# Deformable convolution: a third tap sampled by hat matrices, and ScalarE weighting one of four neighbours

## The chip, the cores and the metric

The kernel runs on one core of a Trainium2 chip. Its engines are TensorE (PE in the profile; its weight loads are shown as PEld), VectorE (DVE), ScalarE (ACT), GpSimd (POOL) and SyncE (SP). Each engine works through its own queue of instructions in order; they meet through semaphores. The metric is the device time of one execution in microseconds (us), lower is better.

## The reference

The whole program is a network of four layers on an image batch `x` of 4 x 128 channels x 64 x 64 positions. The change touches one of its operations only, the deformable convolution of layer 1, which is added to its input after a layer norm over the channels. For each of nine taps k of a 3x3 window, each position has an offset (dy, dx) and a mask, both made by ordinary convolutions; the input is sampled at the shifted position by bilinear interpolation, and the samples are convolved:

```python
off = conv2d(x, w_off, b_off)                       # dy, dx for each of 9 taps
mask = sigmoid(conv2d(x, w_mod, b_mod))
py = oh + ky + dy ;  px = ow + kx + dx
y0 = floor(py) ; x0 = floor(px) ; wy = py - y0 ; wx = px - x0
sampled = v00*(1-wy)*(1-wx) + v01*(1-wy)*wx + v10*wy*(1-wx) + v11*wy*wx
sampled = sampled * mask
out = einsum('bckhw,ock->bohw', sampled, weight) + bias
```

`v00` to `v11` are the four neighbours of the shifted position, zero outside the image. All data are float32.

## The kernel before, in words

**Order of the program.** Phases run one after another: an involution, a recurrence, the deformable convolution, an expert layer, a convolution, a second expert layer, an attention and a last expert layer. The deformable convolution runs from about 1237 to 2453 us of the profiled span. Its work is written between `with tc.manual_schedule(engines=ORDERED)` and the end of the function `deformable`: there each engine's queue has the instructions in the order in which the Python code issues them, so generators that are advanced by `next` set what stands beside what.

**Tiling.** 128 channels lie on the partitions when whole images are held (`xs`, 4 x 4096 positions). An image is cut into 8 chunks of 512 positions, a chunk into 4 tiles of 128. Loops: batch b (4), chunk c (8), gathered tap k (the list `BY_ASK`), pair of tiles i (2). The body of the innermost loop is one step: `taken`, then `step()`.

**Gathered taps.** Seven of nine taps (all but 3 and 4) are gathered. For a pair of tiles `taken` (L993) issues two indirect DMAs from GpSimd (L998); each brings, for 128 positions, the four neighbours' 128 channels from a table in DRAM into a tile `dcn_g` (eight buffers, `GATHERED`). VectorE then multiplies all four neighbours of both tiles by their weights (L1006); the weights of two chunks stand in PSUM (`near_w`, copied at L1160). Two steps' counts later `joined` (L1009) transposes each neighbour on TensorE into one PSUM bank, adding up the four (L1015, 8 joins a pair), so that channels lie on the partitions. When a tap's four tiles are done, `turn_back` (L1118) lets ScalarE copy the bank to `dcn_st` (L1120), and `convolve` (L1123) multiplies by the tap's 128x128 weights into the chunk's output bank (L1127). After the last tap `finish` (L1133) adds it to `xs` on VectorE (L1135). The lags are written in `at(lag, ...)`: join in the step after the gather's, copy three steps after the second pair's, convolution two steps later, finish one more.

**Hat taps.** Taps 3 and 4 (`HATS`) are sampled without a gather by the generator `hats` (L1036), one for each chunk. A tap's sample is written as products with hat functions max(0, 1-|distance|) between a position and the rows and columns near it. `pieces` holds, for each position, a tap's column position and six row weights, each split in three bf16 parts; TensorE transposes them (L1071) and ScalarE copies them to `rowt` (L1075). A small bf16 matmul (`picked`, L1040) spreads one of these rows over 128 partitions in a bank tagged "by"; `across` and `bent` make the column's hat on ScalarE (L1046, L1049, 512 elements each), `weighted` multiplies it on VectorE by the row hat of one of three neighbouring tiles (L1054), which gives a 128x512 square, and `sampled` multiplies four tiles of it on TensorE by `folded` (L1062), which is the image already multiplied by that tap's weights. `fold` (L1027) makes `folded` for one tile: a matmul of the image's tile with the weights of all hat taps side by side (L1030, also in a bank "by") and a scaled copy on ScalarE (L1034). Five tiles are folded ahead of a batch's first chunk, the others at the end of each chunk's generator.

**The plan of the next batch.** A generator `plan(b + 1)` runs beside batch b: layer norm, the offset convolutions (L840), the table of neighbours in DRAM (L818, L820 and DMAs from SyncE), and `places` (L905), which makes indices, weights and `pieces`. It has 123 turns. `step()` (L1137) counts n up, runs what is due in `later`, advances the plan once, and once more where n is a multiple of five, and then advances the first of the generators of hats in `busy` once.

**PSUM.** All eight banks are held: two for joins ("pt"), one output, "pd" and "pv" for the plan, two "by", one for `near_w`.

## Time and profile before

| quantity | value |
|---|---|
| runs of the kernel (three) | 6048.29 median, 6040.84 to 6049.94 us |
| the profiled execution | 6046.03 us, span 6044.2 us |
| busy share of the span | PE 94%, DVE 72%, ACT 56%, POOL 34% |
| first gather issued, last gather issued | 1308.5 and 2444.1 us |
| in the stage 1308 to 2453 us, busy | PE 1057.6, PEld 783.5, DVE 778.4, ACT 341.3, POOL 852.2 us |
| gathers in it (L998) | 896, mean 0.950 us |
| weighting of four neighbours (L1006) | 448, mean 1.214 us |
| joins (L1015) | 3584 |
| gather, from issue to landing | 3.3 / 3.7 / 7.0 us (least, median, most) |

The profile shows one execution. A row of the time line gives start, duration, engine, line, operation, output and inputs, how many like it were put together, and in brackets how long the engine stood idle before it and what ended that. The end of a matmul is modelled and holds its way through the array, so neighbouring rows of PE overlap; the distance from start to start is what a matmul takes from the next. A table of stretches gives for each stretch its length, the busy time of each engine, the TensorE clock that was granted (1.00 is full), the share of the DMA engines and the rate. A line of the table of waits names who waited, for whom, the sum in us, how often, and the longest.

### The profile page before, as it was taken

How to read it: one execution, taken by the hardware profiler on the slowest of the kernel's cores; microseconds unless marked ns; L12 is line 12 of the kernel's file. 1: busy time of each engine (PE TensorE's matmuls, PEld its weight loads, DVE VectorE, ACT ScalarE, POOL GpSimd, SP SyncE). 2: the span in 40 equal slices, each digit the busy share in tenths (PEclk: the TensorE clock that was granted, in tenths of full speed). 3: DMA queues.
4: the chain of work that ended last, by engine and by line, in shares of the span. 5: the costliest groups of instructions: out<-in, count | busy, mean ns of one | idle time of the engine just before them, and what ended most of it. 6: DMA issues, size and time to landing. Idle time of an engine off the chain costs nothing. (4 is left out here: it accounts for less than half of the span.)

```text
span 6044.2 us, 97814 instructions
## 1 busy us (share of the span) xinstructions
PE 5694.5 (94%) x39923; PEld 2247.6 (37%) x39923; DVE 4381.6 (72%) x4739; ACT 3377.4 (56%) x4224; POOL 2057.5 (34%) x2015
## 2 busy tenths in 40 slices
PE   8999999889999988879969999999999999999799
PEld 2222222446667666343333222322232223222233
DVE  6888887456767676356447788878888888888666
ACT  4444444332323322521427888888888888899421
POOL 3889897027777777200000011111111111111000
PEclk9999999989999999989989999999999999999899
DMA  6434432057777777550365566666666666666200
GB/s 215 98 79 85 94 70 47 1 156 230 215 228 220 230 218 211 166 175 0 104 249 121 130 153 147 136 130 150 149 138 130 149 145 142 130 132 132 60 25 27
DMA packets 273147, 818.40 MB, mean 135 GB/s; under 512 B 42612, under 2 KB 100232, under 8 KB 226600
## 3 DMA queue, kind: packets, MB, share of 16 engines
q0 software_dynamic: 109568, 505.75, 35.2%
q1 hardware_dynamic: 163112, 306.20, 17.6%
q8 instruction: 320, 5.24, 0.4%
q14 instruction: 147, 1.20, 0.1%
HBM read 416.71 MB, written 93.13 MB: 84 GB/s over the span
## 5 line engine op out<-in xcount | busy, mean ns | idle before, releaser
L2020 ACT ACTIVATE att_ex<-att_sc,att_shift 128x1024 f32<-128x1024 f32 x2048 | 2141.5, 1111 | 289.7 <-PE att_sc L2016 172.4
L2051 DVE TENSOR_TENSOR att_dve<-att_dve,att_ex 128x2048 f32<-128x2048 f32 x704 | 1631.5, 2317 | 160.9 <-ACT att_ex L2020 135.3
L2016 PE MATMUL att_sc<-att_q,att_k 32*128 32x512 f32 x8192 | 1290.9, 643 | 8.3 <-ACT att_ex L2020 8.3
L2032 PE MATMUL att_pv<-att_ex,att_vals 128*32 128x512 f32 x8192 | 1095.6, 606 | 0.0
L998 POOL DMA_INDIRECT dcn_g<-dcn_table,dcn_idx x896 | 851.3, 950 | 355.4 <-issue 152.9
L412 DVE SCALAR_TENSOR_TENSOR inv_prod<-inv_pk,bspan,inv_seen 128x512 f32<-128x512 f32 (+1 forms) x1120 | 774.6, 743 | 141.6 <-PE inv_pk L399 141.3
L410 POOL TENSOR_TENSOR inv_prod<-inv_seen,inv_prod 128x512 f32<-128x512 f32 (+1 forms) x672 | 837.5, 1274 | 95.5 <-ACT inv_prod L409 95.5
L2049 POOL DMA_DIRECT2D att_dma<-att_ex x224 | 192.5, 859 | 1980.1 <-ACT att_ex L2020 1707.7
L409 ACT ACTIVATE inv_prod<-inv_pk,bspan 128x512 f32<-128x512 f32 (+1 forms) x672 | 436.1, 682 | 505.2 <-PE inv_pk L399 503.8
L2016 PEld LDWEIGHTS att_sc<-att_q,att_k 32*128 32x128 f32 x8192 | 424.9, 183 | 674.8 <-issue 420.0
L1006 DVE TENSOR_TENSOR dcn_g<-dcn_g,dcn_near_w 128x1024 f32<-128x1024 f32 x448 | 538.8, 1214 | 169.8 <-DMA dcn_g<-dcn_table,dcn_idx 153.9
L399 PE MATMUL inv_pk<-inv_red,wtap 32*96 32x512 f32 (+1 forms) x3584 | 512.2, 637 | 7.4 <-DVE wtap L377 7.4
L1015 PE MATMUL dcn_pt<-ident,dcn_g 128*128 128x128 f32 x3584 | 473.6, 276 | 37.2 <-issue 16.4
L1015 PEld LDWEIGHTS dcn_pt<-ident,dcn_g 128*128 128x128 f32 x3584 | 419.3, 142 | 210.6 <-issue 125.1
L421 PE MATMUL inv_out<-inv_prod,inv_fold 96*32 96x512 f32 (+1 forms) x3584 | 478.5, 606 | 8.5 <-DVE xs L429 8.5
L2032 PEld LDWEIGHTS att_pv<-att_ex,att_vals 128*32 128x32 f32 x8192 | 161.5, 108 | 757.4 <-issue 732.2
L399 PEld LDWEIGHTS inv_pk<-inv_red,wtap 32*96 32x96 f32 (+1 forms) x3584 | 131.8, 170 | 386.7 <-DVE inv_prod L412 362.6
L1034 ACT ACTIVATE dcn_fold<-dcn_pf,dcn_turn 128x256 f32<-128x256 f32 x128 | 60.2, 473 | 365.4 <-PE dcn_pf L1030 365.4
L1120 ACT COPY dcn_st<-dcn_pt 128x512 f32<-128x512 f32 x224 | 129.9, 580 | 239.1 <-PE dcn_pt L1015 239.0
L1127 PE MATMUL dcn_out<-dcn_st,dcn_wk 128*128 128x512 f32 x448 | 236.7, 611 | 21.3 <-DVE xs L1135 21.3
L2521 PE MATMUL top_po<-top_xg,top_we 128*128 128x512 f32 x512 | 233.2, 598 | 0.0
L1054 DVE TENSOR_TENSOR dcn_square<-dcn_hx,dcn_by 128x512 f32<-128x512 f32 x192 | 130.1, 678 | 113.5 <-PE dcn_by L1040 86.2
(433 smaller groups left out, 5371.0 us busy)
## 6 DMA issues: line engine op xcount, KB each, us to landing
att_dma<-att_ex POOLq DMA_DIRECT2D x224, 1024.0 KB, 7.4
inv_seen<-inv_image SPq DMA_DIRECT2D x256, 266.0 KB, 9.1
moe_w<-in_L_ffn_weight SPq DMA_DIRECT2D x64, 1024.0 KB, 14.2
att_dma<-att_ex SPq DMA_DIRECT2D x32, 1024.0 KB, 8.6
att_dve<-att_dma POOLq DMA_DIRECT2D x32, 1024.0 KB
moe_table<-moe_xt SPq DMA_DIRECT2D x64, 288.0 KB, 2.8
dcn_table<-dcn_xt SPq DMA_DIRECT2D x32, 512.0 KB, 4.9
dcn_g<-dcn_table,dcn_idx POOLq DMA_INDIRECT x896, 3.7
```

Source lines behind the costliest of these rows:

```text
L399: nc.tensor.matmul(pk[0:m], wtap[half][rg, i, blk], red[rg, h * CH : (h + 1) * CH], start=True, stop=True)
L409: nc.scalar.activation(prod[0:m, h], pk[0:m], AF.Identity, bias=by)
L410: nc.gpsimd.tensor_mul(of, view, of)
L412: nc.vector.scalar_tensor_tensor(out=of, in0=as_shape(pk[0:m], of), scalar=by, in1=view, op0=ALU.add, op1=ALU.mult)
L421: nc.tensor.matmul(po[CR * blk : CR * (blk + 1), h, :], fold[0:m], prod[0:m, h, :], start=unit == 0, stop=unit == UNITS - 1,)
L998: nc.gpsimd.indirect_dma_start(out=g[:, t, :], out_offset=None, in_=rows, in_offset=bass.IndirectOffsetOnAxis(ap=idx[:, Q4 * c + i + t, k ...
L1006: nc.vector.tensor_mul(near, near, by)
L1015: nc.tensor.matmul(pt[0][:, (i + t) * P : (i + t + 1) * P], near[:, t, q, :], net.ident, is_transpose=True, start=i + t + q == 0, stop=i + ...
L2016: nc.tensor.matmul(pes[h // 2][:, h % 2, :], ks[r, t * P : (t + 1) * P], q[r], start=True, stop=True)
L2020: nc.scalar.activation(ex[:, 2 * two : 2 * two + 2, :], pes[two], AF.Exp, bias=shifts[g][:, two : two + 1],)
L2032: nc.tensor.matmul(block["pv"][r], vals[:, t, r], ex[:, h, :], start=t == 0, stop=t == NT - 1)
L2051: nc.vector.tensor_add(block[who], block[who], ex)
```

## The change

A third tap, 5, is moved from the gathered to the hat taps, so that six are gathered: a chunk has 12 steps and not 14. For the gathered ones ScalarE scales the first of the four neighbours of each tile into a new PSUM bank `first` (one buffer, two tiles of 128); VectorE multiplies the other three by their weights (768 elements and not 1024) and adds `first` to the second neighbour (256 elements), so that a tile has three joins and not four. The new bank is taken from "by", which has one. Gather buffers go from eight to seven, buffers of folds from nine to seven, of squares from four to three. A fold is 384 columns wide and not 256, the pieces have 63 rows and not 42.

The generator of hats is written anew: 9 products and not 6, a row is asked for (`picked`) right before its product and no more one ahead, `sampled` follows two products later and not three, turns with nothing in them stand between, and from the third product on it waits until the output bank of the chunk is there. `step()` advances it twice, before and after the rest, and advances the plan a second time where n is a multiple of five or of two. The last convolution of a chunk first runs what is left of the chunk's generator. In `places` the integer copy of the positions shares the buffer of `over`.

```diff
--- before.py
+++ after.py
@@ -597,7 +597,7 @@

-    HATS, PICKED = (3, 4), 7
+    HATS, PICKED = (3, 4, 5), 7

     def __init__(self, net, one, dram):
         tc, nc, ins = net.tc, net.nc, net.ins
@@ -708,8 +708,8 @@
     HATS, PICKED = sampling.HATS, sampling.PICKED
     NH, H0 = len(HATS), HATS[0]
     BY_ASK = [k for k in range(KK) if k not in HATS]
-    BANKS = {"pt": 2, "out": 1, "pd": 1, "pv": 1, "by": 2}
-    GATHERED = 8
+    BANKS = {"pt": 2, "out": 1, "pd": 1, "pv": 1, "by": 1}
+    GATHERED = 7
     tables, woff, boff = sampling.tables, sampling.woff, sampling.boff
     wk, bias, grids = sampling.wk, sampling.bias, sampling.grids
     with ExitStack() as ctx:
@@ -910,7 +910,7 @@
             pieces = sb.tile([P, NT, NH * PICKED, 3], BF16, name="dcn_pieces", tag="dcn_pieces")
             at = slice(H0, H0 + NH)
             for axis in range(2):
-                pos, low, lowi, over = new("pos"), new("low"), new("lowi", I32), new("over")
+                pos, low, lowi, over = new("pos"), new("low"), new("over", I32), None
                 frac.append(new(f"frac{axis}"))
                 nc.vector.tensor_add(pos, grids[axis], off[:, :, axis : 18 : 2])
                 if axis == 0:
@@ -931,6 +931,7 @@
                 nc.vector.tensor_copy(lowi, pos)
                 nc.vector.tensor_copy(low, lowi)
                 yield
+                over = new("over")
                 nc.vector.tensor_tensor(over, low, pos, ALU.is_gt)
                 nc.vector.tensor_sub(low, low, over)
                 yield
@@ -989,8 +990,9 @@
             )

         near_w = ps.tile([P, 2, Q4, KK, 4], F32, name="dcn_near_w", bufs=1)
-
-        def taken(rows, idx, c, k, i):
+        first = ps.tile([P, 2, P], F32, name="dcn_first", bufs=1)
+
+        def taken(rows, idx, w, c, k, i):


             g = sb.tile([P, 2, 4 * P], F32, name="dcn_g", tag="g", bufs=GATHERED)
@@ -1002,8 +1004,13 @@
                     in_offset=bass.IndirectOffsetOnAxis(ap=idx[:, Q4 * c + i + t, k : k + 1], axis=0),
                 )
             near = g.rearrange("p t (q c) -> p t q c", c=P)
-            by = near_w[:, c % 2, i : i + 2, k, :].unsqueeze(3).to_broadcast([P, 2, 4, P])
-            nc.vector.tensor_mul(near, near, by)
+            for t in range(2):
+                nc.scalar.activation(
+                    first[:, t, :], near[:, t, 0, :], AF.Copy, scale=w[:, Q4 * c + i + t, k, 0:1]
+                )
+            by = near_w[:, c % 2, i : i + 2, k, 1:].unsqueeze(3).to_broadcast([P, 2, 3, P])
+            nc.vector.tensor_mul(near[:, :, 1:], near[:, :, 1:], by)
+            nc.vector.tensor_add(near[:, :, 1], near[:, :, 1], first)
             return near

         def joined(pt, i, near):
@@ -1011,13 +1018,13 @@
             if i == 0:
                 pt[0] = ps.tile([P, CH], F32, name="dcn_pt", tag="pt", bufs=BANKS["pt"])
             for t in range(2):
-                for q in range(4):
+                for q in range(1, 4):
                     nc.tensor.matmul(
                         pt[0][:, (i + t) * P : (i + t + 1) * P],
                         near[:, t, q, :],
                         net.ident,
                         is_transpose=True,
-                        start=i + t + q == 0,
+                        start=i + t + q == 1,
                         stop=i + t + q == 6,
                         skip_group_check=True,
                     )
@@ -1030,7 +1037,7 @@
             nc.tensor.matmul(
                 pf[:, 0 : NH * P], net.xs[:, b, tile * P : (tile + 1) * P], cw, start=True, stop=True
             )
-            f = folded[tile] = sb.tile([P, NH * P], F32, name="dcn_fold", tag="dcn_fold", bufs=9)
+            f = folded[tile] = sb.tile([P, NH * P], F32, name="dcn_fold", tag="dcn_fold", bufs=7)
             nc.scalar.activation(f, pf[:, 0 : NH * P], AF.Copy, scale=turned[:, tile : tile + 1])

         def hats(b, c, po, pieces, turned):
@@ -1050,7 +1057,7 @@

             def weighted(k, p):
                 by = bys.pop(0)
-                sq = sqs[k, p] = sb.tile([P, CH], F32, name="dcn_square", tag="dcn_square", bufs=4)
+                sq = sqs[k, p] = sb.tile([P, CH], F32, name="dcn_square", tag="dcn_square", bufs=3)
                 nc.vector.tensor_mul(sq, hxs[k], by)

             def sampled(k, p):
@@ -1073,32 +1080,30 @@
                 )
             rowt = rowts[c % 2]
             nc.scalar.copy(rowt[0:n], pr[0:n])
-            across(0)
             yield
-            bent(0)
-            across(1)
-            yield
+            for k in range(NH):
+                yield
+                across(k)
+                yield
+                bent(k)
             todo = [(k, p) for k in range(NH) for p in range(3)]
-            bent(1)
-            bys.append(picked(sampling.lines[:, 0, 0, :]))
-            yield
+            ahead = [t for t in range(Q4 * c + 5, Q4 * c + 9) if t < NT]
             for m, (k, p) in enumerate(todo):
+                yield
+                while m >= 2 and not po:
+                    yield
+                bys.append(picked(sampling.lines[:, k, p, :]))
                 weighted(k, p)
-                if m + 1 < len(todo):
-                    k1, p1 = todo[m + 1]
-                    bys.append(picked(sampling.lines[:, k1, p1, :]))
-                if m >= 3:
-                    sampled(*todo[m - 3])
+                if m >= 2:
+                    sampled(*todo[m - 2])
+                if m % 2:
+                    yield
+            for i in range(4):
                 yield
-            ahead = [t for t in range(Q4 * c + 5, Q4 * c + 9) if t < NT]
-            for m in range(3, 6):
-                sampled(*todo[m])
+                if i < 2:
+                    sampled(*todo[len(todo) - 2 + i])
                 if ahead:
                     fold(b, ahead.pop(0), turned)
-                yield
-            if ahead:
-                fold(b, ahead.pop(0), turned)
-            yield

         with tc.manual_schedule(engines=ORDERED):
             pw = ps.tile([P, CH], F32, name="dcn_pw", tag="pd", bufs=BANKS["pd"])
@@ -1107,7 +1112,7 @@
             for _ in plan(0):
                 pass
             side = iter(())
-            busy = []
+            busy, hatted = [], {}

             later = {}
             n = 0
@@ -1122,6 +1127,9 @@

             def convolve(k, st, po, b, c):
                 last = k == BY_ASK[-1]
+                if last:
+                    for _ in hatted.pop((b, c)):
+                        pass
                 if k == BY_ASK[0]:
                     po[0] = ps.tile([P, CH], F32, name="dcn_out", tag="out", bufs=BANKS["out"])
                 nc.tensor.matmul(
@@ -1134,16 +1142,20 @@
                 xo = net.chunk(b, c)
                 nc.vector.scalar_tensor_tensor(out=xo, in0=po, scalar=bias, in1=xo, op0=ALU.add, op1=ALU.add)

+            def advance():
+                while busy and next(busy[0], busy) is busy:
+                    busy.pop(0)
+
             def step():
                 nonlocal n
                 n += 1
+                advance()
                 for do in later.pop(n, ()):
                     do()
                 next(side, None)
-                if n % 5 == 0:
+                if n % 5 == 0 or n % 2 == 0:
                     next(side, None)
-                while busy and next(busy[0], busy) is busy:
-                    busy.pop(0)
+                advance()

             for b in range(B):
                 for _ in side:
@@ -1159,7 +1171,8 @@
                 for c in range(NCH):
                     nc.vector.tensor_copy(near_w[:, c % 2], w[:, Q4 * c : Q4 * c + Q4])
                     po = {}
-                    busy.append(hats(b, c, po, pieces, turned))
+                    hatted[b, c] = hats(b, c, po, pieces, turned)
+                    busy.append(hatted[b, c])
                     if c == 2:
                         keep(b, idx, w)
                     if b == 0 and c < B:
@@ -1167,7 +1180,7 @@
                     for k in BY_ASK:
                         pt = {}
                         for i in range(0, 4, 2):
-                            at(2, joined, pt, i, taken(rows, idx, c, k, i))
+                            at(2, joined, pt, i, taken(rows, idx, w, c, k, i))
                             if i:
                                 at(4, turn_back, k, pt, po, b, c)
                             step()
```

## The prediction

> **What bounds the kernel now.** I read first the slices of the page, which put the gathers (POOL at 7 tenths, DMA at 7) between about 1308 and 2453 us, then the stage in four stretches, one for each batch, then its groups of instructions and waits, and last the order of time.
>
> ```profile
> 1308.00:1600.00 292.00, 270.84 (x1774) 197.03 (x1775) 206.05 (x261) 90.09 (x168) 217.08 (x227) 0.96 0.75 223
> 1600.00:1886.00 286.00, 274.16 (x1839) 201.40 (x1838) 199.84 (x248) 90.00 (x168) 213.68 (x225) 0.99 0.75 225
> 1886.00:2170.00 284.00, 270.95 (x1823) 198.36 (x1821) 199.22 (x246) 90.27 (x168) 212.52 (x224) 1.00 0.76 225
> 2170.00:2453.00 283.00, 241.64 (x1559) 186.71 (x1557) 173.30 (x177) 70.91 (x130) 208.88 (x229) 0.96 0.70 206
> ```
>
> Columns after the length: busy PE, PEld, DVE, ACT, POOL, then clock, DMA share, GB/s. Every batch takes 283 to 286 us (the first has 9 us of start in it), although the last has 30 us less PE work, since no next batch is planned beside it. So PE alone can't set the pace there.
>
> ```profile
> 2216.64 0.95 POOL L998 DMA_INDIRECT dcn_g<-dcn_table,dcn_idx  x1 [0.30 <-DMA dcn_g<-dcn_table,dcn_idx]
> 2217.89 0.95 POOL L998 DMA_INDIRECT dcn_g<-dcn_table,dcn_idx  x1 [0.30 <-PE dcn_pt L1015]
> 2219.14 0.95 POOL L998 DMA_INDIRECT dcn_g<-dcn_table,dcn_idx  x1 [0.30 <-issue]
> ```
>
> POOL issues a gather every 1.25 us and the 0.30 between two is there whatever is named as its releaser. A batch has 8 chunks x 7 taps x 4 tiles = 224 gathers: 224 x 1.25 = 280 us. That is the bound of the last batch. In the others PE is just as near:
>
> ```profile
> 1815.72 1.04 PE L1015 MATMUL dcn_pt<-ident,dcn_g 128*128 128x128 f32 x8
> 1816.60 0.60 PE L818 MATMUL dcn_pd<-ident,dcn_pad 128*64 128x128 f32 x4
> 1817.03 1.06 PE L1062 MATMUL dcn_out<-dcn_square,dcn_fold 128*128 128x128 f32 x8
> 1817.92 0.60 PE L1030 MATMUL dcn_pf<-dcn_cw,xs 128*128 128x256 f32 x2
> 1818.36 1.04 PE L1015 MATMUL dcn_pt<-ident,dcn_g 128*128 128x128 f32 x8
> ...
> 1820.56 1.02 PE L1127 MATMUL dcn_out<-dcn_st,dcn_wk 128*128 128x512 f32 x2
> 1821.42 1.04 PE L1015 MATMUL dcn_pt<-ident,dcn_g 128*128 128x128 f32 x8
> ```
>
> Durations hold the drain, so I take the distance of starts: eight joins 0.87 (0.109 each), eight matmuls of the hats 0.89, a fold of 256 columns 0.435, a tap's convolution 0.86; a 512-column bf16 row (L1040) is 0.215 in the same view. No gap: PE is full here, and POOL now and then waits up to 1.75 us for a buffer.
>
> **The change, part by part.** *GpSimd.* One tap of seven is no longer gathered: 32 x 4 = 128 gathers fewer, -160 us of POOL, 192 x 1.25 = 240 a batch. It is worth that only where nothing else takes over.
>
> *PE, one chunk, before:* 112 joins 12.2, 7 convolutions 6.0, 8 rows 1.7, 6 squares x 0.89 = 5.3, 4 folds 1.7, the turned pieces (L1071) 0.4: 27.4, and two waits, for rowt and for xs. Eight chunks are 219; the waits
>
> ```profile
> PE dcn_out L1127 <- DVE xs L1135: 21.3, 17, 2.2
> PE dcn_by L1040 <- ACT dcn_rowt L1075: 21.1, 31, 0.8
> ```
>
> are 5.3 a batch each. The plan of the next batch costs PE 44 (from the same kind of distances: L840 144 x 0.125, L818 64 x 0.11, L792 and L753 eight pairs each at 1.0 and 0.86, the rest 4). Sum 274 against POOL's 280 and 284 measured: two bounds near each other, 4 us over the higher.
>
> *PE after:* 72 joins 7.85 (three of four neighbours, six taps), 6 convolutions 5.2, 12 rows 2.6, 9 squares 8.0, 4 folds of 384 columns 0.65 each (0.435 x 1.5) 2.6, pieces 0.4: 26.6, so 213 a batch. The joins saved (-4.4 a chunk) are nearly all eaten by the third hat tap (+2.7 squares, +0.9 rows, +0.9 folds; one convolution less, -0.9). The rowt wait goes, as a whole step now lies between the pieces and the first row: -5.3. The xs wait stays.
>
> *The bank "by", two to one.* Pieces, rows and folds all pass through it. What is queued behind a blocked one on PE are the joins, and behind those the copy st on ACT, the convolution and the buffers of the gathers. For folds the trace has the cycle of one bank: three rows of the five folds at a batch's start,
>
> ```profile
> 1603.33 3.13 PE L1030 MATMUL dcn_pf<-dcn_cw,xs 128*128 128x256 f32 x10
> 1603.96 0.91 ACT L1034 ACTIVATE dcn_fold<-dcn_pf,dcn_turn 128x256 f32<-128x256 f32 x2 [4.84 <-PE dcn_pf L1030]
> 1604.49 0.73 PEld L1030 LDWEIGHTS dcn_pf<-dcn_cw,xs 128*128 128x128 f32 x4 [0.54 <-ACT dcn_fold L1034]
> ```
>
> from 1603.33 to the third fold's load at 1604.49 and its matmul 0.11 later: 1.27 for a bank to come back, with two banks hiding half. With 384 columns it is 0.2 more on PE and 0.1 to 0.15 more on ACT: about 1.6, of which 0.65 is PE's work: a gate of 0.95. At the batch's start five gates: 4.8. Of the other 27 folds of a batch the third-to-fourth and the fourth-to-pieces follow each other with nothing between, as two turns of the generator meet at a step's border: 13.5 gates, 12.8. Bounds: 0 if PE is waiting anyway, 27 + 5 gates = 30 if every one stands. I take 17.6, counted by the order in the code. Rows wait for the product before them (0.38 row + 0.68 product + some 0.1 = 1.15 against 0.215 + 0.89 of PE's own work): 0.1, twice a chunk, 1.6; upper end below under the slower rival.
>
> PE sum of a planning batch: 213 + 17.6 + 5.3 + 1.6 + 44 = 281.5; of the last 237.5. So POOL's relief moves the bound to PE, which stands where POOL stood. The three planning batches: 281.5 and about 1 to 2 over, single bound now: 283, gain 1 each. The last: max(237.5, 240) and 6 over, since both are near: 246 against 284, gain 38. Sum 41; less 3 for small things that lie bare: places() has 24 columns of pieces more at the start (448 to 672 elements, some 1.5 us before the first row), fold width and the one wider cw matmul. **Gain 38.**
>
> *VectorE.* A pair of tiles was one product of 1024 elements, 1.214. From 0.678 at 512 and 1.214 at 1024: 1.047 ns an element and 0.142 fixed, so 768 cost 0.946 and the sum of 256 costs 0.410: 1.36, 384 of them 521 us against 539. Products of the hats 288 x 0.678 = 195 against 130. DVE 778 to about 830 of 1107: no bound in sum, but 2.46 of about 2.9 us a step while a plan runs (1.36 + 0.51 + 0.5 plan + 0.09). It costs nothing as long as it ends within PE's step.
>
> *ScalarE.* 768 scalings of 128 elements into PSUM. None is in the trace; nearest rows: a 128x128 copy 0.265 (L1479, no scale from a tensor) and 0.473 at 256 with such a scale (L1034). Between 0.265 and 0.473 I take 0.35, as the fixed part of the second row stays when its elements are halved: 204 to 363 us, 270 taken. Third tap's bends 32 x 1.41 = +45, copies -19, wider folds +15: ACT 341 to some 650 of 1107, idle enough. But they are in order: the sum on DVE waits for both scalings, the next scalings wait for that sum (one bank "first"), the copy st stands behind a wait for a gather that came two steps later than its own. Below zero it can't go, as it only adds work and waits. Zero on the path, since DVE already waits for the same gather (153.9 us over the stage), to 0.3 a step, 115 us.
>
> The Trainium skill (ScalarE: Activation LUTs, Rules for kernel authors) speaks against this part: a multiply belongs on VectorE. By its price (What ACT_TABLE_LOAD costs: 186 ns, 93 for a tensor operand, 0.833 an element, back to back 93 less) a scaling would be an estimated 0.29 to 0.39, ACT 220 to 300 more; the sum of the path would stay, as the rows leave ACT idle for over 60% of the stage.
>
> *Buffers.* Eight gather tiles to seven: 7 x 2.5 = 17.5 us of lead against 3.7 landing + some 3 of weighting + one step to the join. Folds nine to seven, six alive: free. Extra columns and lines in the constructor: a few DVE copies beside the recurrence, free. If that cover were gone, under 3 us. Steps call the plan 1.6 times instead of 1.2: 154 calls in 96 steps for its 123 turns, so it still ends within its batch.
>
> **Rivals.** (1) The gates stand beside other waits. PE then needs 213 + 5 + 44 = 262 a batch; gain 22 x 3 + 40 = 106: 5942. For it: PE has 87 us of visible idle time in the stage now; against: in the planning stretches only 10 to 13 a batch. With POOL alone as bound it would be 160, 5888; the 262 exclude it. (2) Slower: a row waits for the whole turn of VectorE. At a step's border DVE has product, sum and hat product in a row (1.36 + 0.68) before the bank is free, and PE only 1.1 of its own. For it: 86.2 us of DVE already spent waiting for these rows, two banks to one; against: in a three-step timetable DVE's chain is about 8.5 of PE's 9.3. Each of 288 rows pays x; 38 us of gain and the 12 of noise are gone at x = 0.17; at 0.5 it is 144, less 38: 6154; about 6100 at 0.3. (3) No change: gains of the last batch given back in the other three by 10 each.
>
> **How the numbers follow.** The profiled execution took 6046 (span 6044.2), 2 below the median of 6048; 6048 - 38 = 6010. The forecast has 0.40 (own range 5985 to 6035), rival 1 0.20, slower 0.28, no change 0.12. Within 0.2% (12 us) is what can't be told from no change. Faster 0.58, same 0.13, slower 0.29. Range 5925 to 6095: down past rival 1, up to a row wait of 0.3.
>
> **What would show it.** Right: 768 gathers, still 1.25 apart in the last batch, which ends in 240 to 250, while the first three stay at 278 to 288 with POOL waiting for joins; ACT-fold as releaser of folds and pieces for 40 to 70 us; rowt gone as a releaser. Wrong: all batches near 262 (gates hidden); or PE's rows waiting for dcn_square for over 50 us, the stage above 1145; or the sums waiting on scalings, and joins on them.

## The result and the profile after

The changed kernel takes **6145.46 us** (median of 4 runs, 6143.36 to 6152.71), the kernel before 6047.19 on the same chip (4 runs). The ratio is 1.0165 with a 95% interval of 1.0154 to 1.0177: slower by 98 us. 6010 were forecast, and the upper end of the range was 6095. The profiled execution took 6147.5 us, with a span of 6145.7.

All of it lies in the gather stage: what comes after it takes 3593 us in the one profile and 3592 in the other. In the stage the batches, counted from the first copy of weights to the next batch's, are

| batch | before | after | forecast |
|---|---|---|---|
| 1 | 283.0 | 309.7 | 283 |
| 2 | 284.6 | 320.2 | 283 |
| 3 | 284.0 | 319.8 | 283 |
| 4 (no plan beside it) | 283.0 | 282.6 | 246 |

So 137 us are missing against the forecast, about 33 in each planning batch and 37 in the last. The stretches of the kernel after, one for each batch (columns as in the prediction: length, busy PE, PEld, DVE, ACT, POOL, clock, DMA share, GB/s):

```profile
1320.00:1630.00 310.00, 271.90 (x1661) 187.90 (x1665) 210.14 (x350) 161.31 (x362) 184.15 (x194) 0.96 0.61 182
1630.00:1950.00 320.00, 279.29 (x1697) 190.72 (x1699) 210.02 (x350) 164.79 (x368) 182.76 (x193) 0.97 0.59 174
1950.00:2270.00 320.00, 278.37 (x1699) 192.13 (x1703) 210.99 (x352) 164.83 (x368) 182.97 (x194) 0.97 0.58 174
2270.00:2552.00 282.00, 243.75 (x1455) 180.88 (x1454) 175.65 (x279) 144.70 (x330) 172.85 (x183) 0.95 0.58 172
```

GpSimd is relieved as planned (183 of 320 us busy; 768 gathers in the stage), yet nothing came of it. PE looks as full as before, 279 us a batch against 274, and that is the trap of this table: a matmul's duration holds its way through the array (a row of 512 columns reads 0.38 us, but the next matmul can start 0.215 after it), and one with nothing close behind it counts that way in full. By the distance of starts PE's own work in a chunk of the last batch is 26.4 us (26.6 were forecast) of the 34.3 that the chunk takes. The rest is mostly waiting. A smaller part is a lower clock: in the second and third batch TensorE was granted 0.97 (above), where it had 0.99 and 1.00 before, and some 20 joins a batch start 0.20 us after the last where 0.109 is usual (4 and none before). An estimate from these clocks, 2 to 3% of the forecast's 257 us of work, is 5 to 7 us a batch. What PE waited for in the stage (total, times, longest):

```profile
PE dcn_by L1047 <- DVE dcn_square L1061: 42.6, 35, 2.3
PE dcn_pf L1037 <- ACT dcn_fold L1041: 36.6, 40, 10.5
PE dcn_pr L1078 <- ACT dcn_fold L1041: 21.4, 32, 0.7
PE dcn_by L1047 <- ACT dcn_hx L1053: 18.6, 26, 1.2
PE dcn_out L1135 <- DVE xs L1143: 8.2, 20, 2.2
```

The wait for rowt (21.1 us before) has gone as forecast. In its place stand four waits for the one bank "by": a row for the product before it, a fold and the pieces for the fold before, a row for the Abs before. How a row comes to wait longer than the product takes is seen in the order of time, in the last batch:

```profile
2425.81 0.95 DVE L1012 TENSOR_TENSOR dcn_g<-dcn_g,dcn_near_w 128x768 f32<-128x768 f32 x1
...
2426.10 0.38 PE L1047 MATMUL dcn_by<-dcn_rowt,dcn_lines 128*128 128x512 bf16 x1
2426.41 0.73 ACT L1056 ACTIVATE dcn_hx<-dcn_hx,dcn_ones 128x512 f32<-128x512 f32 x1
...
2426.57 0.87 PE L1022 MATMUL dcn_pt<-ident,dcn_g 128*128 128x128 f32 x6
2427.04 0.77 ACT L1008 ACTIVATE dcn_first<-dcn_g,dcn_w 128x128 f32<-128x128 f32 x2
...
2427.84 0.42 DVE L1013 TENSOR_TENSOR dcn_g<-dcn_g,dcn_first 128x256 f32<-128x256 f32 x1 [1.08 <-ACT dcn_first L1008]
2428.18 0.68 DVE L1061 TENSOR_TENSOR dcn_square<-dcn_hx,dcn_by 128x512 f32<-128x512 f32 x1
...
2428.91 0.38 PE L1047 MATMUL dcn_by<-dcn_rowt,dcn_lines 128*128 128x512 bf16 x1 [1.47 <-DVE dcn_square L1061]
```

The row of 2426.10 is there by 2426.5. Its product (L1061) stands on VectorE behind a sum (L1013), the sum waits for ScalarE's scalings, and those stand on ScalarE behind a Relu of the hats. So the product starts at 2428.18, and PE, which has only the joins to do in between, waits 1.47 us for the bank. The forecast had 0.1 for this. The waits between ScalarE and VectorE in the stage, and those of GpSimd:

```profile
ACT dcn_first L1008 <- DVE dcn_g L1013: 299.3, 175, 5.8
DVE dcn_g L1013 <- ACT dcn_first L1008: 262.4, 154, 9.1
...
POOL dcn_g L1000 <- PE dcn_pt L1022: 166.1, 90, 8.0
...
POOL dcn_g L1000 <- PE dcn_by L1047: 93.4, 80, 8.4
```

ScalarE and VectorE wait for each other, and GpSimd, which paced the last batch before, now waits for joins to give back its buffers. Before, VectorE waited for gathers:

```profile
DVE dcn_g L1006 <- DMA dcn_g<-dcn_table,dcn_idx: 153.9, 132, 4.9
```

Its product now has no such wait.

The chain of waits, followed back through the second and third batch with the rule by which the profile makes its chain (us in one batch, mean of the two; worked out from the traces):

| on the chain | before | after | two banks, sum in place (below) |
|---|---|---|---|
| PE | 233.5 | 156.4 | 194.5 |
| VectorE | 25.3 | 52.4 | 33.4 |
| ScalarE | 8.1 | 41.2 | 39.7 |
| gathers (GpSimd and DMA) | 6.0 | 38.8 | 20.4 |
| waiting for nothing that the profile shows | 11.2 | 30.3 | 18.6 |
| batch | 284.3 | 320.0 | 307.0 |

Before, PE is 82% of the chain in these two batches and its work can be added up; gathers are 6 us of it, and 114 of 284 only in the last batch, the one that they paced. After, PE is 49%: hand-offs through three engines set the end. The share says what kind of waits there are, not what one is worth: with the sum in place and one bank it is 60% (192 of 319 us), and a planning batch takes as long as with 49%.

### The profile page after: what moved, and what is told of

It is laid out like the page before. It is cut to its first block, busy times and chain, and to the rows that moved or that the text cites. A ratio compares the mean times of both kernels' runs of the same rounds, so it can differ in the third digit from the quotient of the medians.

```text
span 6145.7 us, 98564 instructions
## 1 busy us (share of the span) xinstructions
PE 5716.9 (93%) x39446; PEld 2216.4 (36%) x39459; DVE 4421.1 (72%) x5159; ACT 3677.3 (60%) x5024; POOL 1937.4 (32%) x1887
## 5 line engine op out<-in xcount | busy, mean ns | idle before, releaser
L1000 POOL DMA_INDIRECT dcn_g<-dcn_table,dcn_idx x768 | 731.5, 952 | 561.6 <-PE dcn_pt L1022 166.1
L1008 ACT ACTIVATE dcn_first<-dcn_g,dcn_w 128x128 f32<-128x128 f32 x768 | 283.5, 369 | 337.0 <-DVE dcn_g L1013 299.3
L1013 DVE TENSOR_TENSOR dcn_g<-dcn_g,dcn_first 128x256 f32<-128x256 f32 x384 | 161.7, 421 | 287.4 <-ACT dcn_first L1008 262.4
L1012 DVE TENSOR_TENSOR dcn_g<-dcn_g,dcn_near_w 128x768 f32<-128x768 f32 x384 | 362.9, 945 | 1.1
L1022 PE MATMUL dcn_pt<-ident,dcn_g 128*128 128x128 f32 x2304 | 330.3, 281 | 12.9 <-DVE dcn_g L1013 5.2
L1022 PEld LDWEIGHTS dcn_pt<-ident,dcn_g 128*128 128x128 f32 x2304 | 279.7, 146 | 153.3 <-issue 114.4
L1069 PEld LDWEIGHTS dcn_out<-dcn_square,dcn_fold 128*128 128x128 f32 x2256 | 301.4, 196 | 48.1 <-issue 29.5
L1069 PE MATMUL dcn_out<-dcn_square,dcn_fold 128*128 128x128 f32 x2256 | 303.6, 278 | 0.5 <-issue 0.2
L1061 DVE TENSOR_TENSOR dcn_square<-dcn_hx,dcn_by 128x512 f32<-128x512 f32 x288 | 196.5, 682 | 107.7 <-PE dcn_by L1047 93.1
```

The lines of the kernel that those rows point to most:

```text
L1000: nc.gpsimd.indirect_dma_start(out=g[:, t, :], out_offset=None, in_=rows, in_offset=bass.IndirectOffsetOnAxis(ap=idx[:, Q4 * c + i + t, k ...
L1022: nc.tensor.matmul(pt[0][:, (i + t) * P : (i + t + 1) * P], near[:, t, q, :], net.ident, is_transpose=True, start=i + t + q == 1, stop=i + ...
L1069: nc.tensor.matmul(po[0][:, cols], folded[tile][:, k * P : (k + 1) * P], sq[:, cols], start=False, stop=False, skip_group_check=True,)
```

## The experiments

Theory 1: the one bank for rows, folds and pieces takes the time. Theory 2: the hand-off between ScalarE and VectorE does. The runs fell on chips of two kinds: on the one the kernel before takes 6047 to 6050 us, as above, on the other 6258 to 6276. Every ratio below is to the kernel before on the same chip, and only runs on chips of one kind are set against each other. Most expectations below are written in times of the first kind; where the run fell on the second, what can be held against them is the difference between forms.

### On a chip where before takes 6050 us

**The changed kernel again.** No edit.

> The changed kernel again, beside the following ones, since the kernel before took 6276 us on the chip of the experiments so far and 6047 on the first. Expected: slower than the kernel before by 1.2 to 2.2% (1.65% on the first chip), whatever the chip; with that the single row bank (theory 1) is worth 3% against the version with two banks, which was 1.6% faster than before.

Measured: 6141.25 us, ratio 1.0158 (1.0140 to 1.0176). Batches 309.7, 320.2, 318.2, 280.8. The loss is the same here.

**Sum in place, one bank.** The buffer `first` goes; ScalarE scales the neighbour where it lies.

```diff
-                    first[:, t, :], near[:, t, 0, :], AF.Copy, scale=w[:, Q4 * c + i + t, k, 0:1]
+                    near[:, t, 0, :], near[:, t, 0, :], AF.Copy, scale=w[:, Q4 * c + i + t, k, 0:1]
...
-            nc.vector.tensor_add(near[:, :, 1], near[:, :, 1], first)
+            nc.vector.tensor_add(near[:, :, 1], near[:, :, 1], near[:, :, 0])
```

> As the run before, but one row bank. Theory 1: like the changed kernel, 1.2 to 2% slower than before, as the waits for the bank stay. Theory 2: most of the loss back, within 0.5% of before or faster, as the two mutual waits of 262 and 299 us are cut.

Measured: 6130.29 us, 1.0135 (1.0118 to 1.0152). ScalarE no longer waits for VectorE's sum (VectorE still waits 249 us for the scalings), and the time falls by 11 us, with intervals that overlap; by the batches (306.3, 319.9, 318.8, 267.5) nearly all of it lies in the last one, 13 us. So the 299 us of waits of ScalarE for the sum stood nearly all beside other waits.

**Sum in place, two banks.** As in the run above, and `"by": 2`.

> The changed kernel with the scaled neighbour written back to its place in the gather buffer, so that ScalarE never waits for VectorE's sum, and two row banks. Theory 1 (bank alone): as the version with first in SBUF and two banks, 1.4 to 1.8% faster than before. Theory 2 in part (the hand-off costs the rest): better than that by 0.5% or more, 2 to 3% faster, with ScalarE's waits for the sum gone and VectorE's waits for the scaling under 100 us.

Measured: 6083.12 us, 1.0053 (1.0036 to 1.0070). Batches 299.8, 306.7, 307.2, 256.7. PE's waits with one bank and with two, first one:

```profile
PE dcn_by L1046 <- DVE dcn_square L1060: 43.0, 36, 2.3
PE dcn_pf L1036 <- ACT dcn_fold L1040: 36.6, 40, 10.5
PE dcn_pr L1077 <- ACT dcn_fold L1040: 21.4, 32, 0.7
PE dcn_by L1046 <- ACT dcn_hx L1052: 12.0, 17, 1.1
PE dcn_out L1134 <- DVE xs L1142: 8.4, 21, 2.2
```

and two:

```profile
PE dcn_out L1134 <- DVE xs L1142: 40.7, 23, 2.5
PE dcn_pt L1021 <- ACT dcn_g L1007: 13.9, 10, 2.7
PE dcn_pt L1021 <- ACT dcn_st L1124: 11.3, 12, 1.2
PE dcn_pt L1021 <- DMA dcn_g<-dcn_table,dcn_idx: 10.7, 7, 2.1
PE dcn_pf L1036 <- ACT dcn_fold L1040: 9.8, 1, 9.8
...
PE dcn_by L1046 <- ACT dcn_rowt L1081: 8.9, 17, 2.7
```

The waits for the bank fall from 43.0 + 36.6 + 21.4 + 12.0 = 113 us to 13 (9.8 for the first fold, which the kernel before has too; a row for its product 2.8, 4 times, lower in the list). The time falls by 47, 0.8% of it. The rest comes back in other waits: for xs 40.7 and not 8.4, for scalings, turned tiles and gathers 36 and not 10, for rowt 9. So the second bank is the largest part of the loss that was tested alone, and it is paid in every batch (10 in a planning one, 11 in the last). Both theories had this run faster than the kernel before, and VectorE waiting under 100 us for scalings, the sign that theory 2 asked for, didn't come: it waits 210. 33 us are left against the kernel before, and they lie where the next batch is planned beside the gathers: the three planning batches are 17, 22 and 23 us longer than before, the last is 26 shorter.

**Rows on one bank, folds and pieces on another.** With `first` in SBUF instead of PSUM.

```diff
-    BANKS = {"pt": 2, "out": 1, "pd": 1, "pv": 1, "by": 1}
+    BANKS = {"pt": 2, "out": 1, "pd": 1, "pv": 1, "by": 1, "fo": 1}
...
-        first = ps.tile([P, 2, P], F32, name="dcn_first", bufs=1)
+        first = one.tile([P, 2, P], F32, name="dcn_first", bufs=1)
...
-            pf = ps.tile([P, CH], F32, name="dcn_pf", tag="by", bufs=BANKS["by"])
+            pf = ps.tile([P, CH], F32, name="dcn_pf", tag="fo", bufs=BANKS["fo"])
```

(`pr` in the same way, and six fold buffers for seven.)

> The changed kernel with first in SBUF and the freed PSUM bank given to folds and pieces alone; the rows keep one bank. Of the waits of 5.1 us a chunk on that bank, 1.65 are of folds and pieces and 3.45 of rows. If each is worth what it waits: a third of the gain of two shared banks (a gain of 0.9% on the changed kernel, so within 0.5 to 1% slower than before). If the folds hold up the rest (the copies of them stand between ScalarE's scalings): two thirds or more, 0.3 to 1% faster than before.

Measured: 6130.18 us, 1.0136 (1.0119 to 1.0153), as the in-place form with one bank, and slower than either expectation. The waits of PE and of its weight loads are the old ones:

```profile
PEld dcn_pf L1037 <- ACT dcn_fold L1041: 62.8, 40, 11.1
...
PE dcn_by L1047 <- DVE dcn_square L1061: 44.0, 36, 2.3
PE dcn_pf L1037 <- ACT dcn_fold L1041: 36.6, 40, 10.5
```

The same 40 waits of folds, to the tenth: folds wait for folds, and rows for rows. A second bank split off by kind buys at most the 11 us by which this run lies below the changed kernel; a second one used in turn buys 47.

These 11 us are the same as with the sum in place, though here ScalarE still waits 330 us for the sum. What the two runs share is that `first` has left PSUM. With it in PSUM the two scalings of a pair follow 0.403 us from start to start, with it in SBUF (this run) 0.307, in place 0.292 (medians). For the 96 pairs of the last batch that is 9 to 11 us, which fits the 12 to 13 that this batch gains; that this is the cause isn't shown.

### On chips where before takes 6258 to 6276 us

Here the changed kernel is *faster* than the kernel before (0.9948, at the end of this section).

**Two banks, `first` in SBUF** (the two lines of `BANKS` and `first`, with `"by": 2`; six fold buffers).

> The changed kernel with the scaled neighbour (first) held in SBUF, so that the rows, folds and pieces have two PSUM banks again; a buffer of folds less pays for the SBUF. Theory 1 (the single row bank takes the time): in the changed kernel's last batch TensorE loses 7.65 us a chunk beyond its own work, of which 2.1 waits for the hat product, 1.35 for the bend of a column row, 1.65 for folds and pieces; with two banks most of that 5.1 x 32 = 163 us goes: 5990 to 6040, and waits of rows, folds and pieces under 20 us in sum. Theory 2 (the hand-off between ScalarE and VectorE takes it, 262 and 299 us of mutual waits): they stay, 6125 to 6150.

Measured: 6168.72 us, 0.9838 (0.9822 to 0.9855); the changed kernel, on another such chip, has 0.9948.

**VectorE alone, one bank and two.** ScalarE's scaling and the sum go; one product over four neighbours and four joins, as before; three hats stay (the lines of `first`, of the joins and of `BANKS` aren't shown).

```diff
-            for t in range(2):
-                nc.scalar.activation(
-                    first[:, t, :], near[:, t, 0, :], AF.Copy, scale=w[:, Q4 * c + i + t, k, 0:1]
-                )
-            by = near_w[:, c % 2, i : i + 2, k, 1:].unsqueeze(3).to_broadcast([P, 2, 3, P])
-            nc.vector.tensor_mul(near[:, :, 1:], near[:, :, 1:], by)
-            nc.vector.tensor_add(near[:, :, 1], near[:, :, 1], first)
+            by = near_w[:, c % 2, i : i + 2, k, :].unsqueeze(3).to_broadcast([P, 2, 4, P])
+            nc.vector.tensor_mul(near, near, by)
```

> The changed kernel without ScalarE's scaling: VectorE weights all four neighbours, four joins a tile, three hat taps, still one row bank. TensorE has 24 joins a chunk more, 24 x 0.109 x 32 = 84 us. Theory 1: the row waits stay and TensorE is the bound, 6145 + 60 to 84 = 6205 to 6230. Theory 2: without the hand-off the waits fall to a third, some 4 us a chunk: 6145 + 84 - 130 = 6070 to 6120.

> As the run before, but two row banks. TensorE's own work is 29.0 us a chunk and 5.5 of plan, 32 x 29.0 + 3 x 44 = 1060, against about 1025 before the change. Theory 1: 100 us or more under the run with one bank, near 6070 to 6110, as TensorE's waits are those of the kernel before. Theory 2: within 20 us of the run with one bank.

> The changed kernel without ScalarE's scaling and with two banks: VectorE weights all four neighbours in one product, four joins. Against the in-place form with two banks (6083 us) PE has 24 joins a chunk more, 2.6 us, 21 a batch. Theory 1 (PE's queue bounds, ScalarE costs nothing): 40 to 80 slower than 6083, that is 6120 to 6165, ratio 1.012 to 1.019, last batch 270 to 280. Theory 2 (the chain through ScalarE is what is left over): as fast or faster, 6040 to 6085, ratio 0.998 to 1.006, and PE's share of the chain back in the planning batches above 70 per cent.

> The changed kernel without ScalarE's scaling and with two banks, on the chip of the others of this call. Theory 1 (ScalarE costs nothing; PE has 2.6 us a chunk more joins, 21 a batch): 40 to 80 us slower than the in-place form with two banks, so ratio 1.012 to 1.019 where before is 6050. Theory 2 (the chain through ScalarE is what is left over): no slower than the in-place form, ratio 0.998 to 1.006.

Measured: one bank 6263.28 us, 0.9992 (0.9979 to 1.0005); two banks 6186.22, 0.9867 (0.9850 to 0.9883), and on two other chips 0.9848 (0.9831 to 0.9865) and 0.9856 (0.9838 to 0.9873). The bank is worth 77 us here, without any hand-off from ScalarE: between what theory 2 (within 20) and theory 1 (100 or more) asked for, and nearer to theory 1. And VectorE alone is no faster than the form with ScalarE: 0.9867 against 0.9838 with two banks on one chip, 0.9992 against 0.9948 with one bank, on two chips. So nothing is gained by taking ScalarE's part away. That it costs nothing isn't shown by this: its place is taken by 24 joins a chunk, up to 84 us of PE, and the run can't tell an even exchange from two things that cost nothing.

**The parts alone in the kernel before.** One bank for two, with nothing else (the edit below); ScalarE's scaling in place with three joins, two hats and the old order; and the same with `first` in SBUF.

```diff
-    BANKS = {"pt": 2, "out": 1, "pd": 1, "pv": 1, "by": 2}
+    BANKS = {"pt": 2, "out": 1, "pd": 1, "pv": 1, "by": 1}
```

> The kernel before with one edit: one PSUM bank instead of two for rows, folds and pieces. Theory 1 (the bank): PE in a planning batch has only 10 us to spare, so every gate is paid there; one bank less was worth 47 us with three hats (1.0135 against 1.0053 on one chip), with two hats there are 8 rows a chunk instead of 12, so 30 to 50 us slower: 6080 to 6100, ratio 1.005 to 1.008, planning batches 292 to 300, last batch 283 to 287. Theory 2 (the hand-off between ScalarE and VectorE): the bank is a minor thing without that hand-off: within 12 us of before, ratio 0.998 to 1.002.

> The kernel before with one bank instead of two, on the chip of the others of this call. Theory 1: 30 to 50 us slower where before is 6050 (ratio 1.005 to 1.008), planning batches 292 to 300, last batch 283 to 287. Theory 2: within 12 us, ratio 0.998 to 1.002. On a chip where before is 6258 it was 1.0032 (1.002 to 1.0043).

> The kernel before (two hat taps, two banks, old order of the hats) with one edit: ScalarE scales one of four neighbours in place, VectorE adds it, three joins remain. PE loses 28 joins a chunk, 3.05 us, 24 a batch; GpSimd keeps its 224 gathers, 280 a batch. Theory 1: ScalarE's part costs nothing, GpSimd stays the bound: 6030 to 6055, ratio 0.997 to 1.001, batches 280 to 284. Theory 2: ScalarE waits in its fixed order for gathers and VectorE for ScalarE, so batches lengthen although PE has less to do: ratio 1.004 to 1.012, planning batches 288 to 300, VectorE waiting for ScalarE over 150 us in the stage.

> The kernel before (two hat taps, its generator, two row banks) with only ScalarE's scaling of one neighbour and three joins added, first in SBUF. The gathers (224 x 1.25 = 280 us a batch) remain. Theory 1: nothing lost, TensorE has 28 joins a chunk less, 6030 to 6060. Theory 2: the hand-off costs as in the changed kernel, 6080 to 6150, with VectorE's sum waiting over 200 us for the scaling and TensorE for the sum.

Measured: one bank 1.0032 (1.0020 to 1.0043) and 1.0049 (1.0033 to 1.0064), 19 and 28 us, between what the two theories asked for, where with three hats and VectorE alone it costs 77. ScalarE's part in place 1.0000 (0.9990 to 1.0009), with `first` in SBUF 1.0009 (0.9999 to 1.0018): nothing, though PE has 28 joins a chunk less. Either PE isn't what holds the stage there, or what the joins give ScalarE's part takes; these runs don't tell which.

**Order of rows, and of the weighting.** Both in the form in place with two banks. Rows asked for one product ahead:

```diff
+            bys.append(picked(sampling.lines[:, 0, 0, :]))
             for m, (k, p) in enumerate(todo):
...
-                bys.append(picked(sampling.lines[:, k, p, :]))
                 weighted(k, p)
+                if m + 1 < len(todo):
+                    k1, p1 = todo[m + 1]
+                    bys.append(picked(sampling.lines[:, k1, p1, :]))
```

> The in-place form with two banks, with each row asked for one product ahead, as the kernel before did it (the row of product m+1 is written behind product m, not the row of m right before product m). Theory 1 in its later form (the row's round trip PE to VectorE to PE is still bare although there are two banks): 15 to 35 us faster than 6083 where before is 6050, ratio 0.999 to 1.003 on such a chip, waits of products for rows from 100 us down to 50 or less. Theory 2 (ScalarE's place in the chain): within 12 us of the same form without it, ratio 1.004 to 1.007 on such a chip.

Scaling, product and sum taken out of `taken` into a function `weigh` (not shown), which is due later, and joins and turns one step later:

```diff
-                            at(2, joined, pt, i, taken(rows, idx, w, c, k, i))
+                            near = taken(rows, idx, w, c, k, i)
+                            at(1, weigh, near, w, c, k, i)
+                            at(3, joined, pt, i, near)
                             if i:
-                                at(4, turn_back, k, pt, po, b, c)
+                                at(5, turn_back, k, pt, po, b, c)
```

The edit does less than the expectations below say. `at(1, ...)` falls due in the `step()` that follows `taken`, so the weighting stands in the step of its gather as before, but behind the hats' first turn and the joins, copies and convolutions of that step. Only joins and turns come a whole step later.

> The in-place form with two banks, with the weighting (scaling, product, sum) written one step behind its gather, and joins and turn one step later too. Theory 2 in its form that ScalarE and VectorE stand in their fixed order before a gather that has not landed, with the copy of the turned tile, the hats and the folds behind: 15 to 40 us faster than 6083, so 6043 to 6068, ratio 0.999 to 1.003, DMA on the chain below 5 us a batch. Theory 1: gathers are not what the queue waits for, and seven buffers are held a step longer: 6078 to 6110, ratio 1.005 to 1.010.

> The in-place form with two banks, with scaling, product and sum written one step behind their gather and joins and turn one step later too, on the chip of the others of this call. Theory 2 in the form that ScalarE stands in its order before a gather that has not landed: 15 to 40 us faster than the in-place form, ratio 0.999 to 1.003 where before is 6050. Theory 1: nothing gained, or a loss since seven buffers are held a step longer: ratio 1.004 to 1.010.

Measured: rows ahead 6166.91 us, 0.9832 (0.9816 to 0.9849), the same as two banks with the row asked for late (0.9838; that one has `first` in SBUF). Weighting later in its step 6137.87, 0.9810 (0.9790 to 0.9829), and on the chip of the rows 6151.66, 0.9805 (0.9789 to 0.9821): 15 us less than these, with intervals that just overlap. It is the fastest form on these chips, but its gain is at the small end of what theory 2 asked for, and the new place of the weighting and the later joins weren't tried apart.

**The changed kernel and that fastest form side by side.**

> The changed kernel as it is. On a chip where before is about 6050: 1.015 to 1.018, both theories. On a chip where before is about 6260 to 6280 (its gather stage is some 220 us longer there, at a gather each 1.5 us instead of 1.25): theory 1 says that before is held there by its gathers, which the change cuts by one in seven, and that the one bank eats most of it: two banks gave 0.984 there and one bank cost 0.0125 in the form without ScalarE, so 0.992 to 0.999. Theory 2 says that ScalarE's hand-off costs more where gathers come late: 1.000 to 1.010.

> The in-place form with two banks and the weighting one step behind its gather. On a chip where before is about 6260 to 6280: 0.979 to 0.983, as twice before. On a chip where before is about 6050, against 1.0053 for the same form with the weighting beside its gather: if ScalarE stands in its order before gathers that have not landed, 0.998 to 1.002; if not, 1.003 to 1.010.

Measured: before 6261.11 us; changed 6225.47, 0.9948 (0.9932 to 0.9965); fastest form 6133.85, 0.9795 (0.9778 to 0.9811). It is 92 us below the change, 0.985 of it (0.983 to 0.988 between the ends of their runs), and beats both kernels on chips of this kind. On a chip of the other kind it wasn't run: there the nearest form, with the weighting beside its gather, is 0.5% slower than before.

## Why the prediction was wrong, point by point

**What held.** 768 gathers; rowt gone as a releaser; PE's own work, 26.4 us a chunk in the last batch against 26.6; the durations. From the groups of the kernel after (busy us, mean ns | idle before):

```profile
L1012 DVE TENSOR_TENSOR dcn_g<-dcn_g,dcn_near_w 128x768 f32<-128x768 f32 x384 | 362.9, 945 | 1.1
...
L1008 ACT ACTIVATE dcn_first<-dcn_g,dcn_w 128x128 f32<-128x128 f32 x768 | 283.5, 369 | 337.0 <-DVE dcn_g L1013 299.3 <-DMA dcn_g<-dcn_table,dcn_idx 25.2
...
L1013 DVE TENSOR_TENSOR dcn_g<-dcn_g,dcn_first 128x256 f32<-128x256 f32 x384 | 161.7, 421 | 287.4 <-ACT dcn_first L1008 262.4 <-DVE dcn_g L1012 1.4
```

946, 350 and 410 ns were forecast. The Trainium skill's price for a scaling (ScalarE: Activation LUTs, What ACT_TABLE_LOAD costs), an estimated 0.39 us for one, holds with the 0.369 measured. Its lower end in the prediction, 0.29 in a row, needs an overlap that the trace doesn't show with `first` in PSUM (0.403 from start to start) and does show in place (0.292). Its rule that a multiply belongs on VectorE (same page, Rules for kernel authors), with a reason given for bf16, has no clean test here: with the fp32 tiles and three hats, in the pairs above, the form with ScalarE is 0.3 to 0.4% faster than VectorE alone, but with 24 joins a chunk less, on two chips in one pair and with overlapping intervals in the other. So no instruction was far off its price.

**The step that failed** is the line "PE sum of a planning batch: 213 + 17.6 + 5.3 + 1.6 + 44 = 281.5", with "1 to 2 over, single bound now". The terms of work in it are right as far as the last batch shows them. What is wrong is to take PE's sum for the time of a batch. That was good in the kernel before, where PE is 82% of the chain; after, it is 49%, and a planning batch takes 316.6 us in the mean, 35 over the sum. The price of the bank as a whole was not too low either: 17.6 and 1.6 a batch are 77 us, and on the first kind of chip the second bank is worth 47, on the other 77. Without these gates the sum is 262 a batch; measured with two banks and no `first` are 304.6. So in a planning batch 42 us have no term in the sum: waits, but for some 7 to 10 that the lower clock makes, by the estimate above (0.96 to 0.97 granted there).

**Two terms of it in particular.** "Rows wait for the product before them ...: 0.1, twice a chunk": in six chunks of the last batch PE lost 12.4 us on it by the distance of starts (8.8 of them idle in the profile), 2.1 a chunk, ten times as much, and 1.35 a chunk more on rows that wait for an Abs, which the sum didn't have. Rival 2 had the mechanism, VectorE's turn before the bank comes free. It was argued away with VectorE's 8.5 us of work in PE's 9.3; but work is not the time until the product's turn. And ScalarE was put at "zero on the path": it went from 8 to 41 us of a planning batch's chain, and stays at 40 with two banks. Its queue has scalings, Abs, Relu, folds and turned tiles in one order, and VectorE's sum waits until it has come to the scalings (262 us). The reason given, that VectorE waits for the same gather anyway, overlooked this: VectorE waited for the gather alone. What this wait costs in time was not shown: ScalarE's own wait for the sum could go for 11 us at most.

**The last batch.** max(237.5, 240) + 6 = 246 was forecast. It took 282.6; 267.5 with the sum in place, 256.7 with the second bank as well. So 26 of the 37 us go with these two edits, and this is the only place where a gain then appears, 26 us against before. Here the forecast's mechanism held in part: the relief of GpSimd pays in the batch that gathers paced.

**The rivals.** Slower had 0.28, was priced 6100 at 0.3 us a row and 6154 at 0.5, and came out at 6145, outside the range, which stopped at 0.3. Rival 1 (gates hidden, 5942) is excluded by the second bank's 47 us.

**What stays open.** Of the 33 us that two banks and the sum in place leave on the first kind of chip, the chain puts the most on ScalarE (+32 a planning batch, against -39 on PE); that is a reading, not an experiment. As all that is left lies in planning batches, the faster pace of the plan (1.6 turns a step for 1.2) is a rival to it. It was not tried alone, nor were seven gather buffers for eight, fewer buffers of folds and squares, and most of the new order of the hats.

## What to carry to other kernels

Before summing an engine's work, look at its share of the chain of waits, and remember that this share is one of the kernel before: here it was 82% and fell to 49%. Where a change hands work to engines that stand in a fixed order, the sum is a lower bound and no forecast; here it was 35 us a planning batch too low. Where a PSUM buffer goes from two to one, price it by when the reading engine's queue gets to it, not by how long the read takes: here up to 1.5 us a time and not 0.1. And a wait taken away can be worth far less than the profile shows for it, here 47 us of 100 on PE and 11 at most of 299 on ScalarE, because the next one stands behind it.

## What the runs showed of the hardware

The same program takes 6047 to 6050 us on some chips and 6258 to 6276 on others, and a change that costs 1.6% on the first gains 0.5% on the second. The four chips of the second kind were used at one time each, so that it is the chip and not the moment isn't shown. What comes after the stage takes 3586 to 3601 us on both; nearly all the difference lies where gathers run (for the changed kernel 69 of the 75 us between its profiles on the two kinds). On those of the second kind PE, VectorE and ScalarE stop at once, for up to 4.9 us in the run below and 10.8 in another, and the profile names nothing on this core as the cause. From the last batch of the kernel before with one bank:

```profile
2499.52 0.75 DVE L1135 SCALAR_TENSOR_TENSOR xs<-dcn_out,dcn_bias,xs 128x512 f32<-128x512 f32 x1
2500.51 0.95 POOL L998 DMA_INDIRECT dcn_g<-dcn_table,dcn_idx  x1 [0.30 <-issue]
2501.76 0.95 POOL L998 DMA_INDIRECT dcn_g<-dcn_table,dcn_idx  x1 [0.30 <-issue]
2504.84 0.69 DVE L1054 TENSOR_TENSOR dcn_square<-dcn_hx,dcn_by 128x512 f32<-128x512 f32 x1 [4.57 <-remote]
2504.86 0.58 ACT L1120 COPY dcn_st<-dcn_pt 128x512 f32<-128x512 f32 x1 [9.79 <-remote]
2505.04 0.94 POOL L998 DMA_INDIRECT dcn_g<-dcn_table,dcn_idx  x1 [2.33 <-remote]
...
2505.58 0.59 PE L1040 MATMUL dcn_by<-dcn_rowt,dcn_lines 128*128 128x512 bf16 x1 [5.80 <-issue]
```

From 2500.27 to 2504.84 PE, VectorE and ScalarE all stand still, and GpSimd too for the last 2; the DMA engines go on, with 234 GB/s from 2500 to 2502 and 195 to 2504. Stretches of over 0.8 us in which these three all stand are 51 in that stage, 107 us together; 33 and 75 us with ScalarE's scaling in place in the kernel before; 4 and 7 us in the changed kernel on such a chip; 1 and 2 us in the kernel before on a chip of the first kind. On these chips the runs with seven gathered taps have 33 to 51 of them, those with six 4 to 26. That the change gains there for this reason fits these counts but isn't shown, as the kernel before has no profile on such a chip, and what stops the engines isn't settled.
